# Where the running rows of a gather-and-reduce loop live: SBUF before, a PSUM bank after

## The chip, the cores and the metric

The kernel runs on one core of one Trainium2 chip. The metric is the device time of one launch in microseconds. Five engines work side by side, each through its own queue in order: PE (TensorE, matrix products; PEld are its weight loads), DVE (VectorE), ACT (ScalarE), POOL (GpSimd) and SP, which only issues DMAs. A gather of rows from HBM is issued by POOL, as one indirect DMA of 128 rows.

## The reference, cut to what matters

Two layers of a graph network on 3125 nodes of 256 numbers. Each layer adds, to the nodes' features, an edge part and an attention-like mixing, and then a mixture of experts. The edge part of the first layer takes a maximum over a node's incoming edges, that of the second a sum over messages that were made beforehand, one table for each of 8 relations:

```python
def _L0_gnn_ref(x, src, dst, theta_w, theta_b, phi_w, phi_b):
    theta_x = (x[dst] - x[src]) @ theta_w.T + theta_b
    e = jax.nn.relu(theta_x + x[src] @ phi_w.T + phi_b)
    return jax.ops.segment_max(e, dst, num_segments=x.shape[0])
...
def _L1_gnn_ref(node_feats, src, dst, edge_types, basis, comp, loop_w, h_bias, ln_gamma, ln_beta):
    W = jnp.einsum('rb,bio->rio', comp, basis)
    h_all = jnp.einsum('ni,rio->nro', node_feats, W)
    agg = jax.ops.segment_sum(h_all[src, edge_types], dst, num_segments=node_feats.shape[0])
    h = jax.nn.gelu(agg + node_feats @ loop_w + h_bias + node_feats, approximate=False)
    ...
x = x + _L0_gnn_ref(xn, ...) + _L0_mix_ref(xn, ...)
x = x + _L0_ffn_ref(_layernorm(x), ...)
x = x + _L1_gnn_ref(xn, ...) + _L1_mix_ref(xn, ...)
x = x + _L1_ffn_ref(_layernorm(x), ...)
```

What matters here: for every node, the rows of its neighbours are fetched from a table and reduced, by `max` in the first layer and by addition in the second.

## The kernel before, in words

**Tiles.** The nodes are sorted by their number of edges and lie in 25 tiles of 128. Tile `t` needs `STEPS[t]` rows for each of its nodes (45 for tile 0, 22 for tile 24, 814 in all); row `k` of a tile is one gather of 128 table rows, one for each partition. The source has a preparation, a fast path (`fast`) and a general path that this input doesn't take.

**The stages.** Up to about 100 us the edge lists are sorted and the first table, `btab`, is made. In the first edge pass (to about 1380 us) POOL gathers rows of `btab` (264 numbers: 256 and 8 of bookkeeping) and VectorE takes maxima, while PE and ACT do the mixing of the first layer, until line 1840, and then the first layer's sums, norms and experts. From 1380 to 1640 us the second table `htab_f` is made by 200 wide products. In the second edge pass (to about 2910 us) POOL gathers from `htab_f`, VectorE adds, and PE and ACT do the second layer's attention and its eight experts. Tiles 15 to 18 are `EARLY`: their rows are begun while the table is made and added into `sums` (lines 2140 and 2587), so that the second pass's `edge_pass` has 21 tiles with 696 rows.

**Order.** `edge_pass` (line 1335) writes out the order of VectorE and POOL by hand: after each chunk of rows it takes jobs from a list `bg`, so many units of cost for a row. A job's VectorE part stands in VectorE's queue at that place, and everything behind it waits with it. PE and ACT are not ordered by hand: a planner orders their instructions by what they need.

**The rows before.** In the first pass (`pairs`), the first two rows of a tile go straight into a tile `run` of two rows in SBUF, of which there are two (line 1634). The other rows go, by chunks of 3 or 4, into buffers `gt` (six, line 1714), and after every second row one addition-like operation of 512 numbers takes the pair into `run` (line 1368). Line 1643 saves the bookkeeping numbers of each chunk, line 1393 takes the maximum of `run`'s two halves into `acc`. In the second pass the chunks of 3 or 4 rows go into `gt` (five buffers, line 2012), a tree inside the chunk reduces them to one row (line 1375, first 512 wide, then 256), and line 1377 adds it to `acc`. `acc` begins as the node's own row, which SP loads from `otab` or POOL gathers (lines 2556 to 2561), one tile ahead. All operands of lines 1368, 1375, 1377 and 1393 are in SBUF.

**PSUM.** Four banks are `mm` (`ps_mm`), two belong to `ps_tr`, two to `ps_acc` (tags `acc1` and `acc2`). `ps_tr` serves transposes: a tile's features (line 183), the attention's keys (2268), and in each group of the second pass the two halves of the states (2394), the router's logits (2402, in the same pool) and the weights (2421). ACT copies each out (2270, 2395, 2423), but the logits are read by VectorE (2410). `acc2` holds the mixing's accumulator `pkv` (line 1757) until line 1829 reads it, then a column sum `pmean` (line 1881, which takes `acc1` and `acc2` in turn), and in the second pass the attention's accumulator and the experts' outputs.

**A group of the second pass** (`Group`, line 2310): sums, GELU, two norms in four steps `states_a` to `states_d` that go to and fro between VectorE and ACT, then `routes_a` (transposes and logits), the router's top two, then the experts, whose outputs VectorE takes at line 2482.

Of the kernel before, what the change touches and what calls it, by code (L numbers as in the profile page):

```python
# [99 lines left out]

@with_exitstack
def gps_kernel(ctx: ExitStack, tc: tile.TileContext, a, out):
# [8 lines left out]
    ps_tr = ctx.enter_context(tc.tile_pool(name="ps_tr", bufs=2, space=PSUM))  # L111
# [1207 lines left out]
    def fast():  # L1319
# [15 lines left out]
        def edge_pass(gp, table, wide, idx, op, bg, after, groups, most, pace, own, acc_of, aside, seen=None):  # L1335
# [4 lines left out]
            for g, tiles in enumerate(groups):  # L1340
                accs = []
                left = sum(STEPS[t] for t in tiles)
                for t in tiles:
                    acc = acc_of(t)
                    ids = idx(t)
                    pairs = own is None
                    two = acc[:, :, :D] if pairs else None
                    first = 2 * pairs

                    def fetch_row(dst, k):  # L1350
                        gather(dst, table, ids[:, U - 2 - k : U - 1 - k])

                    if pairs:
                        for k in range(2):
                            fetch_row(acc[:, 1 - k, :], k)
                        seen(t, 0, 0, 2, acc)
                    for i, (k0, k1) in enumerate(chunks(STEPS[t] - first, most)):
                        k0, k1 = k0 + first, k1 + first
                        m = k1 - k0
                        gw = gp.tile([P, most, wide], F32, name="gt")  # L1360
                        gt = gw[:, :, :D]
                        if pairs:
                            for a in range(k0, k1, 2):
                                b = min(a + 2, k1)
                                for k in range(a, b):
                                    fetch_row(gw[:, k1 - 1 - k, :], k)
                                d = two[:, : b - a, :]
                                V.tensor_tensor(d, d, gt[:, k1 - b : k1 - a, :], op=op)  # L1368
                            seen(t, i + 1, k0, k1, gw)
                        else:  # L1370
                            for k in range(k0, k1):
                                fetch_row(gw[:, k1 - 1 - k, :], k)
                            while m > 1:
                                h = m // 2
                                V.tensor_tensor(gt[:, :h, :], gt[:, :h, :], gt[:, m - h : m, :], op=op)  # L1375
                                m -= h
# [1314 lines left out]
```

## Time and profile before

| what | us |
|---|---|
| three timed executions: lowest, median, highest | 2953.78, 2956.93, 2958.68 |
| the profiled execution | 2956.36 |
| its span | 2954.5 |
| PE, weight loads, VectorE, ACT, POOL busy | 1868.2, 1201.3, 1227.5, 556.2, 1718.8 |
| gathers of the first pass into `gt` | 764 x 984 ns |
| gathers of the second pass into `gt` | 742 x 981 ns |
| line 1368, two rows into `run` | 364 x 690 ns, 36 x 425 ns |
| line 1375, the tree | 150 x 683 ns, 214 x 425 ns |
| line 1377, into `acc` | 182 x 428 ns |
| line 2395, ACT's copy of transposed states | 24, median 561 ns |
| mean clock granted to PE | 0.766 |

The span is the profiled execution from its first instruction to its last; the time of a run has a little around it. A line of the timeline gives start, duration, engine, source line, operation, the tiles written and read, and in brackets how long the engine had been idle and what ended that. A line of waits gives who waited for whom, the total in us, how often, and the longest. In a line of groups the two numbers behind the bar are busy time in us and the mean of one in ns, then the engine's idle time before. PE's records are modelled at their ends, and "another core or an unknown queue" is a wait whose releaser the profile couldn't name.

### The profile page before, as it was taken

What the parts mean: (1) busy time and instruction counts of PE and PEld (TensorE: products, weight loads), DVE (VectorE), ACT (ScalarE), POOL (GpSimd) and SP (SyncE); (2) the same over time, 40 slices, a digit from 0 to 9 for tenths busy, and PEclk for the clock granted to TensorE, in tenths of its full rate; (3) what the DMA queues carried; (4) which work ended last, traced back from release to release, by engine and by line L of the source; (5) the groups of instructions that cost most, each with busy time, mean ns of one, the idle gap of its engine ahead of it and who ended that gap; (6) DMA issues with size and microseconds to landing.
All of it is one profiled execution on the core that took longest, in us unless ns stands there. A gap on an engine that the chain in (4) does not pass through costs nothing.

```text
span 2954.5 us, 21207 instructions
## 1 busy us (share of the span) xinstructions
PE 1868.2 (63%) x6161; PEld 1201.3 (41%) x6161; DVE 1227.5 (42%) x3400; ACT 556.2 (19%) x1308; POOL 1718.8 (58%) x1830
## 2 busy tenths in 40 slices
PE   4345666413574635374998267858886886766868
PEld 2223333202342313243443145645554565554657
DVE  7434434434433424334664243335343434343342
ACT  5212221001110101022221122122111122122233
POOL 5566666675667566653146645655666555665651
PEclk9667767655686657687998668878897887887979
DMA  6533333343334233332357432322332222232320
GB/s 180 135 91 86 94 85 104 94 108 101 90 87 107 74 90 85 92 78 58 148 211 237 135 97 75 91 80 84 89 92 85 84 82 79 82 89 73 86 72 18
DMA packets 125963, 290.10 MB, mean 98 GB/s; under 512 B 41386, under 2 KB 63982, under 8 KB 122632
## 3 DMA queue, kind: packets, MB, share of 16 engines
q0 software_dynamic: 83184, 230.02, 28.4%
q1 hardware_dynamic: 38122, 55.88, 5.6%
q10 hardware_dynamic: 4526, 2.71, 0.3%
q8 instruction: 52, 0.85, 0.1%
q14 instruction: 79, 0.65, 0.1%
HBM read 249.07 MB, written 39.41 MB: 98 GB/s over the span
## 4 chain that ended last, share of the span: by engine, by line
PE 25%; issue 9%; another core or an unknown queue 7%; DVE 5%; POOL 4%; ACT 2%; DMA 1%; ACTq 0%; DVEq 0%; SPq 0%; POOLq 0%
PE mm L2432 9%; PE py L2463 7%; PE mm L189 6%; POOL gt L194 4%; DVE gt L1375 1%; PE mm L2326 1%; DVE bnst L163 1%; PE pctx L2271 0%; PE mm L2324 0%; DVE x L2482 0%; PE py L2449 0%; PE pt L2402 0%; DMA gt<-htab_f,idx2g 0%; DVE acc L1377 0%
## 5 line engine op out<-in xcount | busy, mean ns | idle before, releaser
L194 POOL DMA_INDIRECT gt<-htab_f,idx2g x742 | 727.8, 981 | 497.2 <-DVE acc L1377 241.3
L194 POOL DMA_INDIRECT gt<-btab,idx x764 | 751.6, 984 | 389.5 <-issue 208.5
L2432 PE MATMUL mm<-xT,w 128*128 128x256 f32 (+4 forms) x1536 | 429.8, 434 | 107.4 <-issue 61.2
L2463 PE MATMUL py<-w,hT 128*128 128x256 f32 (+1 forms) x1600 | 407.8, 407 | 71.6 <-issue 45.5
L2432 PEld LDWEIGHTS mm<-xT,w 128*128 128x128 f32 x1536 | 294.5, 217 | 224.1 <-issue 121.9
L2463 PEld LDWEIGHTS py<-w,hT 128*128 128x128 f32 (+1 forms) x1600 | 319.8, 203 | 144.1 <-issue 78.9
L1368 DVE TENSOR_TENSOR run<-run,gt 128x512 f32<-128x512 f32 (+1 forms) x400 | 266.3, 666 | 169.6 <-DMA gt<-btab,idx 110.8
L2436 ACT ACTIVATE hT<-mm,b 128x256 f32<-128x256 f32 (+4 forms) x384 | 174.9, 476 | 584.9 <-remote 266.3
L2482 DVE SCALAR_TENSOR_TENSOR x<-py,wf,x 128x256 f32<-128x256 f32 x200 | 88.1, 477 | 440.0 <-remote 226.0
L1375 DVE TENSOR_TENSOR gt<-gt 128x512 f32<-128x512 f32 (+1 forms) x364 | 193.5, 531 | 14.2 <-DMA gt<-htab_f,idx2g 4.9
L1555 PE MATMUL mm<-w,hT 128*128 128x256 f32 x400 | 130.0, 471 | 106.2 <-issue 85.8
L189 PE MATMUL mm<-w_rel,xT 128*128 128x512 f32 x400 | 179.0, 605 | 7.1 <-issue 3.2
L1526 PE MATMUL mm<-xT,w 128*128 128x384 f32 (+2 forms) x320 | 113.8, 519 | 72.8 <-ACT y L1566 34.8
L1555 PEld LDWEIGHTS mm<-w,hT 128*128 128x128 f32 x400 | 90.6, 234 | 158.6 <-issue 123.9
L189 PEld LDWEIGHTS mm<-w_rel,xT 128*128 128x128 f32 x400 | 75.9, 193 | 102.2 <-issue 89.9
L1526 PEld LDWEIGHTS mm<-xT,w 128*128 128x128 f32 x320 | 69.4, 242 | 116.2 <-ACT y L1566 38.4
L1886 PE MATMUL pmean<-ones,xt 128*128 128x1 f32 (+1 forms) x100 | 21.3, 317 | 139.2 <-DVE xt L172 133.7
L189 PE MATMUL mm<-w_qkv,xT 128*128 128x512 f32 (+1 forms) x200 | 90.9, 579 | 25.7 <-issue 19.2
L194 POOL DMA_INDIRECT gt<-htab_f,soon x72 | 71.6, 995 | 44.7 <-issue 20.9
L189 PE MATMUL pt<-w_own,xT 128*128 128x256 f32 x100 | 42.0, 553 | 70.7 <-issue 37.0
L194 POOL DMA_INDIRECT run<-btab,idx x50 | 48.7, 973 | 64.2 <-DVE idx L1630 30.9
L1886 PEld LDWEIGHTS pmean<-ones,xt 128*128 128x128 f32 (+1 forms) x100 | 21.9, 300 | 148.3 <-DVE xt L172 140.9
(440 smaller groups left out, 2221.9 us busy)
## 6 DMA issues: line engine op xcount, KB each, us to landing
htab_f<-hs SPq DMA_DIRECT2D x25, 1024.0 KB
gt<-btab,idx POOLq DMA_INDIRECT x764
gt<-htab_f,idx2g POOLq DMA_INDIRECT x742
w<-in_f_W_dram SPq DMA_DIRECT2D x20, 512.0 KB
ntab<-x SPq DMA_DIRECT2D x5, 640.0 KB
btab<-bs SPq DMA_DIRECT2D x5, 640.0 KB
x<-in_x_dram SPq DMA_DIRECT2D x4, 640.0 KB
otab<-xn SPq DMA_DIRECT2D x16, 128.0 KB
```

What stands on the lines that cost most here:

```text
L163: V.bn_stats(out=st, in_=src)
L189: PE.matmul(ps, lhs[:, c, t * P : (t + 1) * P], w[:, c, :], start=start and c == 0, stop=stop and c == 1)
L194: G.indirect_dma_start(out=dst, out_offset=None, in_=table, in_offset=bass.IndirectOffsetOnAxis(ap=idx, axis=0))
L1368: V.tensor_tensor(d, d, gt[:, k1 - b : k1 - a, :], op=op)
L1375: V.tensor_tensor(gt[:, :h, :], gt[:, :h, :], gt[:, m - h : m, :], op=op)
L1526: PE.matmul(ph[:, :n], w1[:, i, c, f * P : (f + 1) * P], xT[:, c, at0 : at0 + n], start=(c == 0), stop=(c == 1),)
L1555: PE.matmul(py[:, i * D : (i + 1) * D], hTs[i][:, f, j * P : (j + 1) * P], w2[:, i, f, :], start=False, stop=(f == FC - 1), skip_group_che ...
L1886: PE.matmul(pmean[0][:, c : c + 1], xt_tok[:r, t, c * P : (c + 1) * P], ones[:r, 0:1], start=(t in (1, SEEN + 1) and c == 0), stop=(t in ( ...
L2432: PE.matmul(ph[:, :n], w1s[e][:, c, f * P : (f + 1) * P], xT[:, c, at0 : at0 + n], start=(c == 0), stop=(c == 1),)
L2436: S.activation(hT[:, f, :n], ph[:, :n], AF.Gelu, bias=b1[:, e, f : f + 1])
L2463: PE.matmul(py[:r, j * D : (j + 1) * D], hT[:, f, at : at + r], w2s[e][:, f, :], start=(f == 0), stop=(f == FC - 1),)
L2482: V.scalar_tensor_tensor(d, y, wf[:r, t, e : e + 1], d, op0=ALU.mult, op1=ALU.add)
```

## The change

The running rows go to PSUM. In the first pass, once the mixing is done, `run` is a tile of two rows in `acc2`, the bank of the mixing's accumulator; until then it stays in SBUF. In the second pass `run` is in the second of the two banks of `ps_tr`, and everything that used `ps_tr` turns to the first one alone: a small class `Turns` hands out the two tags in turn, and `k` is set to 1 before the second pass and back to 2 behind it. Since `acc2` is taken, both column sums `pmean` use `acc1`.

Both passes now reduce in the same way. All rows go into chunks of at most four (the first may be shorter so that pairs come out even), each pair is taken into `run` by one operation of 512 numbers, which reads `run` in PSUM and the pair in SBUF, and the last pair's result goes to a tile `ends` in SBUF. In the first chunk the pairs are taken together, and an odd row is copied. In the second pass the node's own row and the first gathered row share a tile `begun`, which counts as a pair. The final operation adds the halves of `ends` into `acc`.

```diff
@@ -98,6 +98,16 @@
     return list(zip(at, at[1:]))
 
 
+class Turns:
+
+    def __init__(self, pool):
+        self.pool, self.k, self.n = pool, 2, 0
+
+    def tile(self, shape, dtype, name):
+        self.n += 1
+        return self.pool.tile(shape, dtype, name=name, tag=f"tr{self.n % self.k}")
+
+
 @with_exitstack
 def gps_kernel(ctx: ExitStack, tc: tile.TileContext, a, out):
     nc = tc.nc
@@ -108,7 +118,7 @@
     small = ctx.enter_context(tc.tile_pool(name="small", bufs=6))
     work = ctx.enter_context(tc.tile_pool(name="work", bufs=2))
     ps_mm = ctx.enter_context(tc.tile_pool(name="ps_mm", bufs=4, space=PSUM))
-    ps_tr = ctx.enter_context(tc.tile_pool(name="ps_tr", bufs=2, space=PSUM))
+    ps_tr = Turns(ctx.enter_context(tc.tile_pool(name="ps_tr", bufs=1, space=PSUM)))
     ps_acc = ctx.enter_context(tc.tile_pool(name="ps_acc", bufs=1, space=PSUM))
@@ -1332,7 +1342,7 @@
         comp = bcast_load("comp", a["comp"], 4 * NX, ek)
         br = bcast_load("br0", a["f0_br"], NX, ek)
 
-        def edge_pass(gp, table, wide, idx, op, bg, after, groups, most, pace, own, acc_of, aside, seen=None):
+        def edge_pass(gp, table, wide, idx, op, bg, after, groups, pace, acc_of, run_of, aside, seen=None):
 
 
             credit = 0.0
@@ -1341,56 +1351,46 @@
                 accs = []
                 left = sum(STEPS[t] for t in tiles)
                 for t in tiles:
-                    acc = acc_of(t)
+                    begun, ends = acc_of(t)
                     ids = idx(t)
-                    pairs = own is None
-                    two = acc[:, :, :D] if pairs else None
-                    first = 2 * pairs
-
-                    def fetch_row(dst, k):
-                        gather(dst, table, ids[:, U - 2 - k : U - 1 - k])
-
-                    if pairs:
-                        for k in range(2):
-                            fetch_row(acc[:, 1 - k, :], k)
-                        seen(t, 0, 0, 2, acc)
-                    for i, (k0, k1) in enumerate(chunks(STEPS[t] - first, most)):
-                        k0, k1 = k0 + first, k1 + first
-                        m = k1 - k0
-                        gw = gp.tile([P, most, wide], F32, name="gt")
-                        gt = gw[:, :, :D]
-                        if pairs:
-                            for a in range(k0, k1, 2):
-                                b = min(a + 2, k1)
-                                for k in range(a, b):
-                                    fetch_row(gw[:, k1 - 1 - k, :], k)
-                                d = two[:, : b - a, :]
-                                V.tensor_tensor(d, d, gt[:, k1 - b : k1 - a, :], op=op)
-                            seen(t, i + 1, k0, k1, gw)
-                        else:
-                            for k in range(k0, k1):
-                                fetch_row(gw[:, k1 - 1 - k, :], k)
-                            while m > 1:
-                                h = m // 2
-                                V.tensor_tensor(gt[:, :h, :], gt[:, :h, :], gt[:, m - h : m, :], op=op)
-                                m -= h
-                            V.tensor_tensor(acc, own(t) if i == 0 else acc, gt[:, 0, :], op=op)
+                    run = run_of()
+                    n, own = STEPS[t], begun is not None
+                    odd = (n + own) % 2
+                    cuts_ = [0] + list(range(4 - odd - own, n, 4)) + [n]
+                    for i, (k0, k1) in enumerate(zip(cuts_, cuts_[1:])):
+                        gw = gp.tile([P, 4, wide], F32, name="gt")
+
+                        def rows_of(a, b):
+                            return gw[:, k1 - b : k1 - a, :D]
+
+                        for k in range(k0, k1):
+                            dst = begun[:, 1, :] if own and k == 0 else gw[:, k1 - 1 - k, :]
+                            gather(dst, table, ids[:, U - 2 - k : U - 1 - k])
+                            if i and (k - k0) % 2:
+                                V.tensor_tensor(ends if k == n - 1 else run, run, rows_of(k - 1, k + 1), op=op)
+                        if i == 0:
+                            if odd:
+                                one = begun if own else rows_of(0, 2)
+                                V.tensor_tensor(run[:, 0, :], one[:, 0, :], one[:, 1, :], op=op)
+                                V.tensor_copy(run[:, 1, :], rows_of(k1 - 1, k1)[:, 0, :])
+                            else:
+                                V.tensor_tensor(run, begun if own else rows_of(0, 2), rows_of(k1 - 2, k1), op=op)
+                        if seen is not None:
+                            seen(t, i, k0, k1, gw)
                         if t == 0 and i == 3:
-                            d = two[: P // 2, 0, :] if pairs else acc[: P // 2, :]
+                            d = run[: P // 2, 0, :]
                             V.tensor_tensor(d, d, spill, op=op)
 
                         rate = min(max(sum(c for c, _ in bg) / left, pace[0]), pace[1])
-                        n1 = k1 - (k0 if i else 0)
-                        left -= n1
-                        credit = min(credit, 0.0) + rate * n1 if bg else 0.0
+                        left -= k1 - k0
+                        credit = min(credit, 0.0) + rate * (k1 - k0) if bg else 0.0
                         aside()
                         while bg and credit > 0.0:
                             cost, job = bg.popleft()
                             job()
                             credit -= cost
-                    if pairs:
-                        acc = accp.tile([P, D], F32, name="acc")
-                        V.tensor_tensor(acc, two[:, 0, :], two[:, 1, :], op=op)
+                    acc = accp.tile([P, D], F32, name="acc")
+                    V.tensor_tensor(acc, ends[:, 0, :], ends[:, 1, :], op=op)
                     if t == NT - 1:
 
                         pj = ps_mm.tile([P, 512], F32, name="mm")
@@ -1631,7 +1631,14 @@
 
             def begin0(t):
                 rows_asked(t)
-                return l0w.tile([P, 2, ROW], F32, name="run", bufs=2)
+                return None, l0w.tile([P, 2, D], F32, name="ends")
+
+            mixed = []
+
+            def run0():
+                if mixed:
+                    return ps_acc.tile([P, 2, D], F32, name="run", tag="acc2")
+                return l0w.tile([P, 2, D], F32, name="run")
 
             places = l0w.tile([P, U], F32, name="places")
             G.iota(places, pattern=[[-1, U]], base=0, channel_multiplier=0, allow_small_or_imprecise_dtypes=True)
@@ -1839,6 +1846,7 @@
                 yield
                 V.tensor_copy(u_mix, pu.rearrange("p (m d) -> p m d", m=2))
                 m0x.close()
+                mixed.append(True)
                 begin()
@@ -1878,7 +1886,7 @@
                     V.reciprocal(self.rs[:, : self.k], self.rs[:, : self.k])
                     for j, t in enumerate(self.tiles):
                         if t in (1, SEEN + 1):
-                            pmean[0] = ps_acc.tile([P, 2], F32, name="pmean", tag=f"acc{1 + (t > 1)}")
+                            pmean[0] = ps_acc.tile([P, 2], F32, name="pmean", tag="acc1")
                         normalize(xt_tok[:, t, :], x[:, t, :], self.mv[:, j, :], self.rs[:, j : j + 1])
                         V.tensor_tensor(x[:, t, :], x[:, t, :], bet, op=ALU.add)
                         r = rows(t)
@@ -1954,8 +1962,8 @@
 
             with tc.manual_schedule(engines={mybir.EngineType.DVE, mybir.EngineType.Pool}):
                 edge_pass(
-                    gp, btab[:], ROW, idx1.get, ALU.max, bg, after0, GROUPS, 4, (0.9, 1.3), None,
-                    begin0, ahead, seen0,
+                    gp, btab[:], ROW, idx1.get, ALU.max, bg, after0, GROUPS, (0.9, 1.3),
+                    begin0, run0, ahead, seen0,
                 )
                 while bg:
                     bg.popleft()[1]()
@@ -2212,6 +2220,7 @@
                 w1s[e] = mat_load(f"w1_{e}", a["f1_W1"][e], pool, F, nc.sync)
                 w2s[e] = mat_load(f"w2_{e}", a["f1_W2"][e], pool, D, nc.sync)
 
+            ps_tr.k = 1
             kx = ExitStack()
             kp = kx.enter_context(tc.tile_pool(name="kp", bufs=1))
             w1qkv = mat_load("w1qkv", a["m1_qkv"], kp, 3 * P, nc.sync)
@@ -2554,17 +2563,20 @@
             inits, order1 = {}, [t for tiles in GROUPS1[2:] for t in tiles]
 
             def load_init(t):
-                inits[t] = accp.tile([P, D], F32, name="acc")
+                inits[t] = fin.tile([P, 2, D], F32, name="begun", bufs=2)
                 if t in owns:
-                    gather(inits[t], h_rows, own_i[:, t : t + 1])
+                    gather(inits[t][:, 0, :], h_rows, own_i[:, t : t + 1])
                 else:
-                    nc.sync.dma_start(inits[t], otab[t * P : (t + 1) * P, :])
+                    nc.sync.dma_start(inits[t][:, 0, :], otab[t * P : (t + 1) * P, :])
 
             def begin1(t):
                 i = order1.index(t) + 1
                 if i < len(order1):
                     load_init(order1[i])
-                return inits[t]
+                return inits[t], fin.tile([P, 2, D], F32, name="ends")
+
+            def run1():
+                return ps_tr.pool.tile([P, 2, D], F32, name="run", tag="tr1")
 
             def first_groups():
@@ -2600,11 +2612,12 @@
                 first_groups()
                 edge_pass(
                     gp, h_rows, D, lambda t: idx2[:, t, :], ALU.add, bg, lambda g, *a: after1(g + 2, *a),
-                    GROUPS1[2:], 4, (0.9, 1.3), lambda t: inits[t], begin1, aside,
+                    GROUPS1[2:], (0.9, 1.3), begin1, run1, aside,
                 )
                 while bg:
                     bg.popleft()[1]()
                     flush()
+        ps_tr.k = 2
         fx.close()
 
     unfit = nc.values_load(flag[0:1, 0:1])
```

## The prediction

> **What bounds the kernel now.** I read the totals and the chain of waits first, then windows cut where the passes begin and end, then the waits of each engine inside them, then the timeline around single gathers. The windows:
>
> ```profile
> core 0: us, PE busy (x) PEld busy (x) DVE busy (x) ACT busy (x) POOL busy (x), PEclk, DMA share, GB/s
> 100.00:491.00 391.00, 210.38 (x578) 108.84 (x578) 157.40 (x539) 82.03 (x305) 254.56 (x259) 0.71 0.36 95
> 491.00:1380.00 889.00, 435.21 (x1240) 262.08 (x1241) 341.77 (x921) 86.02 (x185) 568.29 (x579) 0.67 0.35 92
> 1380.00:1640.00 260.00, 217.55 (x550) 102.23 (x548) 147.78 (x388) 52.68 (x118) 104.78 (x106) 0.92 0.55 190
> 1640.00:2912.00 1272.00, 929.06 (x3419) 667.98 (x3420) 504.13 (x1307) 272.96 (x541) 743.99 (x758) 0.81 0.29 82
> ```
>
> 491 us is where the mixing ends (the copy of line 1840); only after it does the change put the first pass's running rows in PSUM. A gather takes 0.95 us and leaves 0.30 before the next, so 579 of them need 724 of the 889 us: no engine is full in the first pass, but POOL is nearest. In the second pass (1640 to 2912) PE works 929 us of 1272. The waits say which of two engines is late:
>
> ```profile
> DVE run L1368 <- DMA gt<-btab,idx: 110.8, 65, 2.9
> POOL gt L194 <- DVE slots L1643: 55.8, 13, 11.4
> ...
> DVE gt L1375 <- DMA gt<-htab_f,idx2g: 4.9, 2, 3.1
> POOL gt L194 <- DVE acc L1377: 241.3, 49, 12.5
> PE pt L2394 <- DVE hh L172: 60.5, 9, 13.7
> PE pt L2402 <- ACT xT L2395: 39.9, 8, 15.0
> ```
>
> In the first pass VectorE waits for rows 65 times, and at other times POOL waits for a buffer (17 idle stretches over 0.45 us after 491 us, 149 us together). In the second VectorE hardly waits for a row, while POOL stands 241 us behind line 1377: a faster gather has almost nobody waiting for it there.
>
> What the change touches on POOL is seen where a gather starts inside an addition:
>
> ```profile
> 1020.87 0.69 DVE L1368 TENSOR_TENSOR run<-run,gt 128x512 f32<-128x512 f32 x1 [2.45 <-remote]
> 1021.10 1.27 POOL L194 DMA_INDIRECT gt<-btab,idx  x1 [0.30 <-issue]
> 1022.68 0.95 POOL L194 DMA_INDIRECT gt<-btab,idx  x1 [0.30 <-issue]
> ...
> 2679.82 0.88 DVE L2482 SCALAR_TENSOR_TENSOR x<-py,wf,x 128x256 f32<-128x256 f32 x2 [1.33 <-PE py L2463]
> 2680.01 0.95 POOL L194 DMA_INDIRECT gt<-htab_f,idx2g  x1 [0.30 <-issue]
> ```
>
> The gather at 1021.10 is held until the addition with two SBUF inputs ends at 1021.56, and takes 1.27 us. The one at 2680.01 starts inside an operation whose other tensor lies in PSUM, in the operand order that the change uses, and takes 0.95. Gather by gather, what is above 0.945 us comes to 22.2 us after the mixing, 15.1 of it (73 gathers) beside line 1368, and to 26.0 us in the second pass, 18.4 beside lines 1375 and 1377.
>
> **The change part by part.** (1) Relief of the gathers: 15.1 us of POOL time in the first pass, 18.4 in the second. How much reaches the end? In the first pass, the gathers that VectorE waits for: 65 waits of two rows, 130 of 578, 22%: 3.4 us. In these stretches an addition starts 0.4 us into a gather and is over before the next, so the held gathers lie mostly where VectorE catches up and POOL later waits anyway. In the second pass the chain has 3.5% of the span (103 us of 1272, 8%) on gathers: 1.5 us. Bounds: nothing, or all of it in the first pass. **-5 us**.
>
> [...]
>
> (2) Run-ahead in the first pass: before, the first two rows of a tile go into a tile of their own (two such), beside six buffers; after, every row passes through the six. A buffer holds 3.82 rows before (764 in 200) and 3.80 after (814 in 214). A stall's run-ahead of about 23 rows crosses a tile's start 0.7 times (32.6 rows a tile), so POOL stands still 0.7 x 2 x 1.25 = 1.75 us earlier in each of 17 stalls, 30 us, of which the same 22% counts: **+7**. Bounds 0 and 30.
>
> (3) VectorE's work: in the second pass 150, 214 and 182 operations (102.5 + 91.0 + 78.0 = 271.5 us) become by the cuts 333 of 512 elements at 0.690, 30 of 256 at 0.425 and 9 copies at about 0.42 (an estimate from the 256-wide row): 246 us. The chain holds 42.7 us of lines 1375 and 1377, 16% of their work, so 25 us less is **-4**. Bounds 0 and -25. In the first pass 315.5 us become 318; nothing, hidden by the 200 us and more that VectorE waits for PE and ACT.
>
> The price of a PSUM operand: these rows have their tensors in SBUF (1368, 1375) and one in PSUM (2474):
>
> ```profile
> L1368 DVE TENSOR_TENSOR run<-run,gt 128x512 f32<-128x512 f32 x364 | 251.1, 690 | 158.4 <-DMA gt<-btab,idx 108.6 <-remote 26.4 <-DVE run L1368 8.4
> L1375 DVE TENSOR_TENSOR gt<-gt 128x512 f32<-128x512 f32 x150 | 102.5, 683 | 5.1 <-DMA gt<-htab_f,idx2g 4.9
> L2474 DVE TENSOR_TENSOR x<-x,py 128x512 f32<-128x512 f32 x9 | 6.2, 687 | 24.1 <-PE py L2449 18.0 <-PE py L2463 6.1
> ```
>
> Reading costs nothing. VectorE never writes PSUM here: bounds by the slowest and fastest 512-wide rows, 751 ns (line 1584) and 497 (line 1580), +61 and -193 on some 600 operations, +37 and -116 us, at 16% +6 and -19. I take 690, since the nearest row differs by memory only.
>
> [...]
>
> (4) One transposing bank in the second pass. Line 2394 transposes a group's two halves into two banks and ACT copies each (line 2395, median 0.56 us) while PE goes on. With one bank the second half's transposes wait for the first copy, and the logits of line 2402, in the same bank, for the second: two copies in series with PE, 1.1 us and two hand-overs, 1.2 a group. PE waits at line 2402 for ACT in 8 of the 12 groups: **+10**. Lower bound 0, other matmuls being put between. Upper: in three groups (ended at 2226.8, 2500.6, 2610.0) the chain has 20.5, 15.3 and 10.9 us between the states and ACT's copy, with PE out of work; were each repeated by the added hand-over, +47. The 25 transposes of line 2268 run in pairs, 1.76 us for two tiles. With one bank a tile costs 0.27 + 0.37 + 0.05 if the next transpose goes ahead of the product, as now, or 0.27 + 0.37 + 0.56 = 1.2 if not: between 0 and 0.32 x 25 = 8, **+4**, on the chain throughout.
>
> (5) Nothing: both column sums in acc1 (the second waits for the guess's copy of the first, which line 1448 awaits anyway; without that cover, the 23.0 us PE waits there). The own rows go into two `begun` buffers in place of `acc`, free once the tile before has done its first addition; SP's and POOL's loads keep their place in the queues. The single `run` and `ends` are touched by VectorE alone, in order, so nobody queues behind them.
>
> Sum: -5 + 7 - 4 + 10 + 4 = **+12 us** on the profiled execution's 2956.4 (span 2954.5 and 1.9 around it, 0.6 below the runs' median): **2968 us**.
>
> **Rivals.** *The relief reaches the end:* POOL is nearest to full in the first pass, and a chain there would pass all 15.1 us on; with VectorE's 4 and 1.5, and the bank and run-ahead hidden, 2956.4 - 21 = **2936**. Against it: 241 us of POOL waiting. *It cancels:* the planner, which orders PE and ACT itself, puts other matmuls between the halves: -5 + 7 - 4 = -2, **2955**. *The bank runs PE dry:* term 4 at +47 in place of +10, **3005**, decided once PE has no queued matmul at three or more of the hand-overs. *The lock stays:* the gathers remain long, the change not doing what it is built for: 2968 + 5 = **2973**; the row at 2680.01 speaks against it.
>
> **How the numbers follow.** Chances: +12 as summed 0.36, relief 0.32, cancelling 0.16, PE dry 0.11, lock 0.05. A measurement here can tell 0.2%, 6 us. Slower is the first, fourth and fifth less 0.04 of the first that falls within 6 us: 0.48; same 0.16 + 0.04 = 0.20; faster 0.32. The likeliest's own range, terms 1 to 3 each moved half way to their bounds (-8 to +28 in all), is 2948 to 2984; for 8 in 10 it reaches to the relief on one side and most of the way to PE dry on the other: 2930 to 2996.
>
> **What would show it.** Gathers of the first pass after the mixing near a mean of 0.955 us (now 0.982) show the relief; POOL's idle before them growing shows the run-ahead; additions at 690 ns the PSUM price; line 2394 waiting for ACT about once a group the bank. A second pass shorter than 1272 us by over 10 makes term 4 wrong, a first pass shorter by over 10 terms 1 and 2.

## The result, and the profile after

| | lowest, median, highest us |
|---|---|
| before, 6 runs | 2943.35, 2952.01, 2958.68 |
| the change, 6 runs | 2971.44, 2987.45, 3008.82 |

The change is slower: its time is 1.0128 of the time before, 95% interval 1.0096 to 1.0159, or 38 us (28 to 47). The forecast was +12 us, 2968, with a range of 2930 to 2996. The direction and the range hold; the size is three times the forecast. The profiled execution took 2983.25 us, its span is 2981.4, 26.9 more than before.

The windows of the changed kernel, cut at the same events as those before (the end of the mixing, the last gather of the first pass, and 18 us after the first gather of the second pass); the columns are as there:

```profile
100.00:479.00 379.00, 213.89 (x576) 112.99 (x577) 159.33 (x540) 82.08 (x305) 253.85 (x257) 0.71 0.37 97
479.00:1396.00 917.00, 427.72 (x1223) 252.85 (x1221) 344.07 (x908) 82.94 (x179) 557.86 (x581) 0.66 0.34 90
1396.00:1662.00 266.00, 224.84 (x561) 107.47 (x560) 147.36 (x388) 53.69 (x121) 102.93 (x106) 0.91 0.51 176
1662.00:2938.00 1276.00, 931.62 (x3433) 665.31 (x3434) 484.38 (x1137) 278.18 (x545) 728.40 (x758) 0.81 0.29 84
```

By this one execution the first pass after the mixing lost 28 us (889 to 917), the table 6, and the second pass only 4 (1272 to 1276). In the second pass PE and ACT are busy 3 and 5 us more than before, VectorE and POOL 20 and 16 less: no engine has much more work, so what is lost is idle time. A second profile of the same kernel put the loss elsewhere (experiment 1), so the split of one execution is not to be trusted here.

The groups of the changed kernel, by line and shape (busy us, mean ns, idle before):

```profile
L1370 DVE TENSOR_TENSOR run<-run,gt 128x512 f32<-128x512 f32 x639 | 445.2, 697 | 135.5 <-DMA gt<-btab,idx 49.9 <-remote 42.5 <-issue 18.6
L1370 DVE TENSOR_TENSOR ends<-run,gt 128x512 f32<-128x512 f32 x46 | 31.7, 689 | 18.8 <-DMA gt<-btab,idx 7.3 <-DMA gt<-htab_f,idx2g 5.0 <-issue 2.5
L204 POOL DMA_INDIRECT gt<-btab,idx x814 | 789.0, 969 | 481.4 <-issue 222.5 <-DVE slots L1650 121.4 <-DVE idx L1630 73.1
L204 POOL DMA_INDIRECT gt<-htab_f,idx2g x721 | 693.4, 962 | 508.0 <-issue 193.4 <-DVE run L1370 189.0 <-DVE sums L2599 45.3
```

Two things were as forecast. An operation with its running rows in PSUM takes 697 ns and not 690. And the gathers are no longer held: 981 ns became 962 in the second pass; in the first, the gathers after the mixing go from 983 to 961 (the 969 includes those before it). What was not forecast is that the time grew although both of these rows are right.

### The profile page after: what moved, and what is told of

Read it like the earlier page. It is cut to its first block, busy times and chain, and to the rows that moved or that the text cites. A ratio compares the mean times of both kernels' runs of the same rounds, so it can differ in the third digit from the quotient of the medians.

```text
span 2981.4 us, 21020 instructions
## 1 busy us (share of the span) xinstructions
PE 1878.4 (63%) x6161; PEld 1201.0 (40%) x6161; DVE 1211.5 (41%) x3218; ACT 557.8 (19%) x1308; POOL 1690.2 (57%) x1830
## 4 chain that ended last, share of the span: by engine, by line
PE 27%; issue 8%; another core or an unknown queue 7%; DVE 6%; ACT 2%; POOL 1%; DMA 0%; ACTq 0%; DVEq 0%; POOLq 0%
PE mm L2441 9%; PE py L2472 8%; PE mm L199 6%; DVE run L1370 2%; PE pctx L2280 1%; POOL gt L204 1%; DVE bnst L173 1%; DVE x L2491 1%; PE py L2458 1%; ACT hT L2445 0%; PE pt L2411 0%; PE mm L2335 0%; PE pt L2403 0%; DVE x L2376 0%
## 5 line engine op out<-in xcount | busy, mean ns | idle before, releaser
L204 POOL DMA_INDIRECT gt<-btab,idx x814 | 789.0, 969 | 481.4 <-issue 222.5
L204 POOL DMA_INDIRECT gt<-htab_f,idx2g x721 | 693.4, 962 | 508.0 <-issue 193.4
L1370 DVE TENSOR_TENSOR run<-run,gt 128x512 f32<-128x512 f32 x639 | 445.2, 697 | 135.5 <-DMA gt<-btab,idx 49.9
L2472 PE MATMUL py<-w,hT 128*128 128x256 f32 (+1 forms) x1600 | 411.9, 406 | 109.1 <-issue 64.2
L2441 PE MATMUL mm<-xT,w 128*128 128x256 f32 (+4 forms) x1536 | 418.6, 427 | 82.4 <-ACT hT L2445 34.7
L1526 PE MATMUL mm<-xT,w 128*128 128x384 f32 (+2 forms) x320 | 130.2, 570 | 193.8 <-issue 94.3
L1555 PE MATMUL mm<-w,hT 128*128 128x256 f32 x400 | 108.7, 428 | 12.5 <-issue 10.7
L1555 PEld LDWEIGHTS mm<-w,hT 128*128 128x128 f32 x400 | 83.0, 214 | 49.9 <-issue 35.0
L194 ACT COPY xT<-pt 128x256 f32<-128x256 f32 x100 | 36.2, 375 | 282.5 <-issue 142.2
L1876 DVE TENSOR_TENSOR acc<-acc,pt 128x256 f32<-128x256 f32 x25 | 10.4, 417 | 173.2 <-PE pt L199 115.4
L2403 PE MATMUL pt<-ident,hh 128*128 128x128 f32 x50 | 15.6, 402 | 85.7 <-DVE hh L182 33.4
```

The costliest lines, as they stand in the source:

```text
L194: S.copy(xT[:, :, t * P : (t + 1) * P], pt)
L204: G.indirect_dma_start(out=dst, out_offset=None, in_=table, in_offset=bass.IndirectOffsetOnAxis(ap=idx, axis=0))
L1370: V.tensor_tensor(ends if k == n - 1 else run, run, rows_of(k - 1, k + 1), op=op)
L1526: PE.matmul(ph[:, :n], w1[:, i, c, f * P : (f + 1) * P], xT[:, c, at0 : at0 + n], start=(c == 0), stop=(c == 1),)
L1555: PE.matmul(py[:, i * D : (i + 1) * D], hTs[i][:, f, j * P : (j + 1) * P], w2[:, i, f, :], start=False, stop=(f == FC - 1), skip_group_che ...
L2441: PE.matmul(ph[:, :n], w1s[e][:, c, f * P : (f + 1) * P], xT[:, c, at0 : at0 + n], start=(c == 0), stop=(c == 1),)
```

## The experiments

Ratios are to the kernel before, timed in turn with it on the same chip. Experiments 1 to 4 ran on one chip, 5 to 8 on a second, 9 and 10 on a third, 11 and 12 on a fourth; where two kernels of different chips are compared, it is by their ratios. "Second pass" below, where a length is given for it, means the time from line 2300 of the changed kernel (the attention's last product, on VectorE) to the last addition into `x`, in the one profiled execution of each.

**1. The change again.** No edit.

> The changed kernel, unaltered, for a second profile and more times. The sum of the prediction (one transposing bank and run-ahead as the costs): about 2987 us, and the second pass (from the first of its gathers to the end) longer than before by 10 us or more. The regrouping theory (the new cuts of the chunks move VectorE's jobs, and the order of PE and ACT with them; memory has no part in it): about 2987 us, and again 20 to 40 us more than before between the end of the mixing and the last gather of the first pass, with the second pass within 5 us of before.

2999.19 us, 1.0192 (1.0148 to 1.0237). The loss is real, but its place moved: between the end of the mixing and the last gather of the first pass this profile has 896 us, against 917 in the first one and 887 before. The regrouping theory, formed after the first profile, expected 20 to 40 us there in every execution; it has 9.

**2. Running rows of the first pass back in SBUF.**

```diff
-                if mixed:
-                    return ps_acc.tile([P, 2, D], F32, name="run", tag="acc2")
                 return l0w.tile([P, 2, D], F32, name="run")
```

> The changed kernel with the running rows of the first pass in SBUF throughout; VectorE's, POOL's and ACT's instructions in the same order. The sum of the prediction: the gathers of the first pass are held again (mean 983 ns in place of 961), of which 3.4 us reach the end: 2990 us. Relief in full: 2999. If writing PSUM from VectorE, or the bank taken from the column sums, cost the time: 2955 to 2965. The regrouping theory: 2987, within 5 us.

2987.50 us, 1.0119 (1.0069 to 1.0169). The first pass's gathers are held again, as expected (mean 988 ns after the mixing). Most of the loss is still there: 35 us, of 57 in experiment 1, which ran on the same chip, and of 38 in the result.

**3. Running rows of the second pass back in SBUF, and two transposing banks.**

```diff
-            ps_tr.k = 1
...
-                    run = run_of()
+                    run = run_of() or ends
...
-                return ps_tr.pool.tile([P, 2, D], F32, name="run", tag="tr1")
+                return None
```

> The changed kernel with the running rows of the second pass in SBUF (in the tile that holds the last pair) and both transposing banks back in turn. The sum of the prediction: 14 us less for the bank and 1.5 more for the gathers: 2974. The bank running PE dry: 2940 to 2950. The regrouping theory: 2987, within 5 us.

2956.96 us, 1.0014 (0.9974 to 1.0054). The loss is gone but for 4 us (-8 to 16), so most of it belongs to the second pass's half of the change.

**4. Both passes in SBUF.** Edits 2 and 3 together; VectorE's and POOL's instructions stand in the same order as in the changed kernel.

> The changed kernel with the running rows of both passes in SBUF and both transposing banks: what is left is the new cuts of the chunks, the pairs, the lost tiles for the first rows. The sum of the prediction: run-ahead +7 and VectorE's lesser work -4, 2955. The regrouping theory: 2980 to 2995, all of the loss without any PSUM.

2930.85 us, 0.9965 (0.9931 to 0.9999): a little faster than before. The regrouping theory falls here. The new cuts, the pairs, `begun` and both column sums in `acc1` are all in this kernel, and together they cost nothing. Between this kernel and experiment 3 lies only the memory of the first pass's rows: 0.0049, or 14 us for rows in PSUM, with intervals that touch.

**5. The kernel before with one transposing bank in its second pass.**

```diff
+            ps_tr.k = 1
             kx = ExitStack()
```

(with the class `Turns` from the change).

> The kernel before with one transposing bank in its second pass and nothing else. The sum of the prediction: +14 us, 2964. If the bank is what makes the second pass of the changed kernel longer: +40 or more, 2990. If it is the memory of the running rows instead: within 5 us of before.

2966.06 us, 1.0034 (1.0001 to 1.0067), +10 us. This is the bank as the prediction summed it (+14), and far from the 40 that would explain the result.

**6. Both passes in SBUF, one bank.** Experiment 4 with `ps_tr.k = 1` kept.

> The changed kernel with the running rows of both passes in SBUF, but one transposing bank in the second pass: between it and e3_both_sbuf (2931 us) lies the bank alone, between it and e1_run0_sbuf (2987) the memory of the rows alone. Bank: 2970 to 2990. Memory of the rows: 2928 to 2940. Both by halves: about 2958.

2948.93 us, 0.9987 (0.9959 to 1.0015). The bank costs 0.0022 against experiment 4 (6.5 us; 18 by the medians). From here to experiment 2 (1.0119, on the other chip) it is 0.0132, 39 us; with experiment 4, which shares experiment 2's chip, it is 0.0154 for bank and rows together, 45 us. Between these two kernels VectorE, POOL and SP have the same instructions in the same order, and PE and ACT differ in four places where a few of the experts' instructions change order: what differs is that the second pass's running rows lie in PSUM. The new order doesn't explain the loss: at the first of the four places experiment 2 has already lost 32 of the 44 us that it loses from the start of the second pass on (and 38 of 44 in the pair of experiments 10 and 9 below, which differs in the same places).

The timeline shows where the bank's part is. The attention's transposes, two banks (experiment 4), then one (this one); start, duration, engine and line, tiles, count, idle before:

```profile
1684.22 0.38 PE L2274 MATMUL pt<-ident,kT 128*128 128x128 f32 x2
1684.59 0.62 ACT L2276 ACTIVATE ks<-pt,rs 128x128 f32<-128x128 f32 x2 [1.02 <-PE pt L2274]
1685.02 1.13 PE L2277 MATMUL pctx<-x,ks 128*128 128x256 f32 x4 [0.41 <-ACT ks L2276]
```

```profile
1683.82 0.42 PE L2275 MATMUL pt<-ident,kT 128*128 128x128 f32 x1
1684.34 0.37 ACT L2277 ACTIVATE ks<-pt,rs 128x128 f32<-128x128 f32 x1 [1.59 <-PE pt L2275]
1684.76 1.22 PE L2278 MATMUL pctx<-x,ks 128*128 128x256 f32 x2 [0.52 <-ACT ks L2277]
1685.78 0.42 PE L2275 MATMUL pt<-ident,kT 128*128 128x128 f32 x1
```

With two banks a pair of tiles goes through together; with one, each tile takes its own turn, 1.95 us in the median. Against experiment 4 this stage (first transpose to last product) is 11.3 us longer here, between 10.8 and 12.0 in the change, in experiment 1 and in experiment 2, and 13.0 and 37.5 in experiments 9 and 10 (the latter stage began 20 us earlier); in those with the change's order and two banks it is the same to 0.1. The groups' transposes (the other user of the bank) added little: 1193.7 us for the second pass against 1188.4 here, 1225.1 against 1225.2 in experiment 5.

**7. Rows of the second pass in PSUM, but transposes turning between two banks again.** Experiment 2 with

```diff
-                        pt = ps_tr.tile([P, 512], F32, name="pt")
+                        pt = (ps_mm.tile([P, 512], F32, name="mm") if c else ps_tr.tile([P, 512], F32, name="pt"))
...
-                pt = ps_tr.tile([P, 2, P], F32, name="pt")
+                pt = ps_mm.tile([P, 2, P], F32, name="mm") if t % 2 else ps_tr.tile([P, 2, P], F32, name="pt")
```

> e1_run0_sbuf (rows of the second pass in PSUM, 2987 us) with every second transpose of the attention and the second half of a group's states in a bank of ps_mm, so that transposes turn between two banks again. Bank: 2940 to 2960. Memory of the rows: 2980 to 2990.

2962.09 us, 1.0033 (1.0006 to 1.0060): between the two expectations. By the ratios it gives 25 us back against experiment 2 and stays 20 above experiment 4. Both parts are there; neither is the whole. (The edit also puts transposes into the banks of `mm`, and PE's order differs from experiment 4's in some 20 places, so this pair is less clean than the one before.)

**8. Five row buffers in the first pass in place of six.** Experiment 4 with `bufs=5`.

> e3_both_sbuf (2931 us) with five row buffers in the first pass in place of six: 3.8 rows of run-ahead less. By the prediction's term 2 (1.4 rows lost cost 7 us): 17 stalls x 3.8 rows x 1.25 us x 22% = +18 us, 2949. If run-ahead isn't worth anything in the first pass: 2926 to 2936.

2942.60 us, 0.9934 (0.9900 to 0.9968). A whole buffer less, 3.8 rows, costs nothing that can be measured: experiment 4, on the other chip, has 0.9965, and the intervals overlap. (Against this kernel, on its own chip, experiment 7 is 0.0099 slower, 29 us.) Run-ahead is worth nothing here.

**9 and 10. POOL slowed down again.** After every second gather of the second pass, a memset of one column, in experiment 2 (rows in PSUM) and in experiment 6 (rows in SBUF):

```diff
                             gather(dst, table, ids[:, U - 2 - k : U - 1 - k])
+                            if own and k % 2:
+                                G.memset(spare, 0.0)
```

> e1_run0_sbuf (rows of the second pass in PSUM, one bank, 2987 us) with a memset of 128x1 on POOL after every second gather of the second pass, 0.09 us each, some 350 of them: POOL gets back about the 28 us that the shorter gathers saved it; VectorE's, PE's, ACT's and SP's instructions keep their order. If the loss comes from POOL's shorter gathers (rows earlier, and what that collides with): back to 2949 or little more. If it comes from VectorE's operand in PSUM itself: 2985 to 3000.

> e5_sbuf_one_bank (rows in SBUF, one bank, 2949 us) with the same memsets: what the memsets cost by themselves. By the 441 us that POOL waits for VectorE in the second pass: 2945 to 2955. If POOL's time counts in full: 2980.

With rows in PSUM 3028.54 us, 1.0218 (1.0182 to 1.0254); with rows in SBUF 2990.31, 1.0106 (1.0068 to 1.0145). So it isn't the shorter gathers that hurt: making POOL slow again did not bring the time back, it made it worse. And the pair, on one chip, repeats the distance of experiments 6 and 2: 0.0112, 33 us, for rows in PSUM. The second finding was expected by nobody: 342 memsets of 118 ns, 40 us of POOL time, cost 29 us with rows in PSUM (against experiment 2) and 35 with rows in SBUF (against experiment 6), by ratios from different chips, although POOL waits long for VectorE in this pass (180.5 us behind line 1370 in experiment 6, 212.2 in experiment 2). Either POOL's time counts nearly in full there, or the memsets disturb something else; no run tells these apart.

The second pass in all these profiles (a count from the traces, us):

```
kernel                         second pass  PE busy  PE idle  POOL busy
before                              1225.2    931.6    293.6      704.9
5  before, one bank                 1225.1    938.3    286.9      707.3
4  SBUF, two banks                  1188.4    927.9    260.5      717.0
8  SBUF, two banks, 5 buffers       1201.8    928.0    273.8      719.4
3  SBUF, two banks, PSUM in first   1209.2    925.9    283.3      714.9
6  SBUF, one bank                   1193.7    921.4    272.3      716.0
10 SBUF, one bank, memsets          1219.3    930.9    288.4      757.5
7  PSUM, two banks                  1225.6    934.4    291.1      688.6
2  PSUM, one bank                   1237.2    933.9    303.4      688.5
   the change                       1221.7    923.0    298.7      690.8
1  the change again                 1230.1    927.8    302.3      690.7
9  PSUM, one bank, memsets          1263.6    938.0    325.6      728.6
```

Of the kernels with the change's cuts and pairs (all but the first two of the table), every one with rows in SBUF and no memsets is below 1210, every one with rows in PSUM above 1220, though POOL saves 28 us of gathers in the latter. PE's work is the same to 2%; its idle time grows. The operations next to the rows don't tell why: VectorE's operation ends and POOL's gather starts 0.270 us later in both (median of the waits for the row operation), an ACT operation of 128x256 (the experts' hidden layer) takes 471 to 472 ns in all of them, and the matmuls of the experts' second product start 0.216 us apart at the full clock and 0.427 at half of it (medians), beside a running-row operation or not, in experiments 6 and 2 alike. The windows of the second pass in experiments 6 and 2, one fence each, give the same:

```profile
1735.00:2929.00 1194.00, 922.34 (x3524) 669.94 (x3523) 473.60 (x1131) 275.06 (x544) 716.00 (x719) 0.84 0.29 84
```

```profile
1737.00:2974.00 1237.00, 933.58 (x3519) 679.38 (x3519) 474.17 (x1130) 273.96 (x544) 688.61 (x720) 0.83 0.28 81
```

VectorE 474 us in both, POOL 27 less, PE 11 more at a clock of 0.83 in place of 0.84, and 43 us more in all. What does differ is the place of the idle time. The clock granted to PE is either 1.0 or 0.5 in the records. Matmul by matmul, experiment 2 loses 206 us against experiment 6 at those that only it meets at the half clock, regains 193 at those that only the other meets so, and loses 26 at the rest. A stretch at the half clock looks like this one of the changed kernel's PE timeline, with the window around it:

```profile
2113.78 0.59 PE L2472 MATMUL py<-w,hT 128*128 128x256 f32 x1 [2.31 <-issue]
2115.18 0.58 PE L2472 MATMUL py<-w,hT 128*128 128x256 f32 x1 [0.81 <-issue]
2116.59 0.58 PE L2472 MATMUL py<-w,hT 128*128 128x256 f32 x1 [0.82 <-issue]
2118.68 0.58 PE L2472 MATMUL py<-w,hT 128*128 128x256 f32 x1 [1.51 <-issue]
2121.48 0.59 PE L2472 MATMUL py<-w,hT 128*128 128x256 f32 x1 [2.22 <-issue]
```

```profile
2111.00:2135.00 24.00, 7.38 (x12) 3.55 (x13) 0.43 (x1) 2.06 (x3) 15.50 (x17) 0.51 0.33 97
```

Matmuls that elsewhere follow each other after 0.216 us, or 0.427 at the half clock, start 1.40, 1.41, 2.09 and 2.80 us apart, all near multiples of 0.70. No releaser is shown for these waits ("issue"), but the granted clock is low: 0.51 over the stretch. Of such starts (a wait of the kind "issue", at least 1.35 us after the matmul before, within 0.02 of a multiple of 0.70) the changed kernel's profile has 87, 69 of them wholly at the half clock; before has 60 and 47.

Do they explain the loss? In the second pass these starts take 83 us in experiment 2 against 79 in 6, 113 in 7 against 96 in 4, and 121 in 9 against 77 in 10; the time at the half clock is 429 us against 385, 420 against 406, and 445 against 428. The losses of the three pairs are 43, 37 and 44 us. Neither count gives all three, so by what rows in PSUM cost time stays open. The last two runs, on another chip, show what a profile without such starts looks like.

**11. The kernel before with only the first pass's rows in PSUM,** in its own order, with its own tile for the first rows:

```diff
-                                d = two[:, : b - a, :]
-                                V.tensor_tensor(d, d, gt[:, k1 - b : k1 - a, :], op=op)
+                                w = b - a
+                                src = (two if a == first else run)[:, :w, :]
+                                d = (two if b == STEPS[t] else run)[:, :w, :]
+                                V.tensor_tensor(d, src, gt[:, k1 - b : k1 - a, :], op=op)
```

(`run` is a tile in `acc2` once the mixing is done, and `two` until then; the column sums are both in `acc1`.)

> The kernel before with its first pass's running rows in the mixing's bank once the mixing is done: a tile's first pair is read from the tile in SBUF and written to PSUM, the last pair's result goes back to SBUF; both column sums in acc1. Chunks, buffers, own tile for the first rows and the order of all engines stay as before, and the second pass is untouched. The prediction's term 1 (relief, 15.1 us of POOL time, 22% of it reaching the end): 3 us faster, within 0.2% of before. Relief in full: 15 us faster. If rows in PSUM cost as in the second pass (some 0.13 us for each of the operations, of which there are some 270 after the mixing): 25 to 45 us slower.

**12. The kernel before with the pairs in its second pass only,** rows in SBUF, two banks: experiment 4's second pass behind the first pass of before.

> The kernel before with the pairs, the new cuts and begun in its second pass only, rows in SBUF, two transposing banks: the change's second pass without PSUM, behind the first pass of before. If what makes e3_both_sbuf and e8_five_buffers faster than before (0.9965 and 0.9934 of it) lies in the second pass alone, as their second passes of 1284 and some 1295 us against 1324 say: 0.990 to 0.995 of before. By the prediction's term 3: 4 us, 0.9986.

These two ran on another chip than all others, and there the kernel before takes 2454.86 us (2451.32 to 2459.46, 18 runs) in place of some 2955. On it, experiment 11 takes 2446.63 us, 0.9967 (0.9955 to 0.9978): rows in PSUM in the first pass are 8 us faster (5 to 11). Experiment 12 takes 2449.59 us, 0.9977 (0.9968 to 0.9986), 6 us faster.

The profile of experiment 11 is another world. Its groups:

```profile
L194 POOL DMA_INDIRECT gt<-btab,idx x764 | 737.9, 966 | 232.7 <-issue 192.2
L194 POOL DMA_INDIRECT gt<-htab_f,idx2g x742 | 729.1, 983 | 227.6 <-issue 196.8
L2469 PE MATMUL py<-w,hT 128*128 128x256 f32 (+1 forms) x1600 | 379.6, 392 | 45.4 <-DVE x L2488 45.4
L1380 DVE TENSOR_TENSOR gt<-gt 128x512 f32<-128x512 f32 (+1 forms) x364 | 194.8, 535 | 266.3 <-DMA gt<-htab_f,idx2g 253.7
```

and its waits after the mixing:

```profile
DVE runp L1373 <- DMA gt<-btab,idx: 334.4, 208, 2.8
```

POOL's idle time is its own 0.30 us between gathers and little else; VectorE waits 334 us for rows in the first pass and 254 in the second, where the trace of before had 110.8 and 4.9. No wait of this execution is put down to an unknown releaser, and the matmuls of line 2469 have no idle time of the kind "issue" (64.2 us for the same line in the changed kernel's profile). The clock of this chip is another, too; the spans and mean clocks of experiment 11 and of the kernel before in its first profile:

```profile
core 0: 2443.3 us, clock 0.829
core 0: 2954.5 us, clock 0.766
```

Experiment 11 spends 835 us at the half clock and 1608 at the full one, before on its own chip 1382 and 1573: the 511 us between them lie in the time at the half clock. Experiments 11 and 12 have none of the starts on the grid of 0.70 us, though they too run a third of their time at the half clock. On this chip POOL is at a gather or in the 0.30 us behind it nearly all the time: in experiment 11 its 555 instructions from 400 to 1100 us and the 0.30 behind each make 698 of the 700 us (531 of them busy), and the 794 from 1360 to 2400 us make 1020 of 1040 (782 busy). Shorter gathers paid about in full in its first pass (8 us, 5 to 11, for the 7 counted below). The new cuts and pairs of the second pass pay as well; by what isn't shown, since VectorE, whose work they lessen, waits for rows there (297.5 us in experiment 12). The gathers of the first pass after the mixing average 960 ns here and 973 in experiment 12, which has its rows in SBUF: 554 x 13 ns are 7 us, and 8 were gained. The changed kernel itself was not run on this chip. Whether it is faster there is open.

Of the kernels tried, those of experiments 8 and 4 were the fastest on the slower chips (0.9934 and 0.9965 of before, intervals that overlap, against 1.0128 and 1.0192 for the change), and those of experiments 11 and 12 were the two tried on the faster one (0.9967 and 0.9977).

## Why the prediction was right in sign and wrong in size

**The relief of the gathers (-5).** The mechanism is right: the mean fell to 961 and 962 ns in the two passes, near the 955 that the prediction asked for. Its worth was read from POOL's waits: 241 us of waiting, so "a faster gather has almost nobody waiting for it". That reading is weak. Experiments 9 and 10 charged most of 40 us of POOL time to the end (if a memset costs nothing else), and experiment 11 passed about all of 7 us on, on a chip where POOL does not wait. On the slower chips the relief can't be seen: with the first pass's rows in PSUM the kernel was 14 us slower, not faster (experiments 4 and 3, intervals that touch).

**Run-ahead (+7).** Wrong: nothing that shows. The term counted with 1.4 rows less of run-ahead in each stall; experiment 8 took 3.8 rows away, nearly three times as much, and lost nothing (9 us less by the ratios, give or take 14, against the 18 that the term would give). So a share of POOL's stalls can't be priced here by the share of gathers that VectorE waits for.

**VectorE's lesser work (-4).** Right in sign; -10 (-20 to 0) for all new cuts and pairs of both passes in experiment 4, -6 (-8 to -3) for the second pass alone in experiment 12. That VectorE's time is what was saved isn't shown.

**The price of a PSUM operand (0).** This is the step that failed. "I take 690, since the nearest row differs by memory only": the row was right, 697 ns, and with it the bound of +6 was kept. But the price doesn't stand in the row's duration. With the same order of VectorE and POOL, rows of the second pass in PSUM cost 39 us (experiments 6 and 2), 33 (10 and 9) and 20 (4 and 7, with two banks), net of the gathers that they shorten. The prediction bounded an operation's price by the durations of other operations; it had no term for what such an operation does to the others. The mechanism by which it does so isn't shown. That it has to do with the half clock and the starts on the grid of 0.70 us is a conjecture: there the kernels drift apart, but neither count gives the loss in all three pairs; and on the chip without such starts rows in PSUM were a gain, but in the first pass of another kernel, so that the two were never compared on one chip.

**One bank (+14).** The sum was right: +10 (0 to 20) in experiment 5, +6.5 in experiment 6. The split was not. The attention took +11 in place of +4: the next transpose does not go ahead of the product, and a tile costs 1.95 us, beyond the 1.2 that the upper bound allowed. (25 tiles at 1.95 in place of 0.88 would be 27 us more; the stage grew by 11. With two banks three of its steps take 6.2, 10.6 and 10.0 us in the trace of before, with PE idle for 3.3, 6.8 and 7.5 of them; that one bank hides most of this idle time is an estimate, from the 27 and the 11.) The twelve groups took 0 to 5 in place of 10. PE does wait there as forecast, about once a group:

```profile
PE pt L2403 <- ACT xT L2404: 28.8, 10, 18.0
```

But these waits hardly lengthen the pass: experiment 6 has them too (10 times, 9.1 us), and its second pass is 5 us longer than that of experiment 4, where two profiles of one kernel differ by 8 (the change and experiment 1).

**Nothing for `pmean`, `begun` and `ends`.** Experiment 4 contains all three and isn't slower than before.

**The sum** of what was measured: -10 (new cuts and pairs) + 39 (rows of the second pass, beside one bank) + 6.5 (bank) + 3 to 22 (rows of the first pass, experiment 2 against the change's two ratios) = 38 to 57, against 38 and 57 for the two sets of the change; each step begins where the one before ends, so the sum must come out, and it is no independent proof. Of the rivals, "the lock stays" (2973) and "the bank runs PE dry" (3005) lie 14 and 18 us from the result, nearer than the forecast's 19, and both for a wrong reason: the gathers were freed, and the bank cost less than its sum. "The relief reaches the end" is what the other chip shows for the first pass. That the result lies in the stated range is luck: the likeliest's own range (2948 to 2984) misses it, and the wider one held it by reaching towards "PE dry", which did not happen.

## What to carry to other kernels

In this kernel an operation's own duration didn't price where it reads and writes (697 ns against 690, but 20 to 39 us for the pass): put back one memory at a time, with the order of the queues unchanged, before believing a row that "costs the same". Where a profile has much idle time without a releaser, its shares can say little about what a microsecond of an engine is worth (here POOL had 241 us of waiting in the second pass, and 40 us more of its time cost 29 and 35): look at the granted clock in those stretches, and slow that engine by a known amount. And this kernel took 2454.86 us on one chip and 2950 to 2963 on three others, so a change should be timed on more than one.

## What the runs showed of the hardware that was not expected

- The kernel before takes 2454.86 us on one chip and 2950 to 2963 on three others, with medians that repeat. The slower ones have stretches in which PE starts matmuls at multiples of 0.70 us in place of 0.216 or 0.427 (87 such starts in the changed kernel's profile, 69 of them at the half clock), and waits without a known releaser (252 us of VectorE's in the second pass of experiment 6); the profiles of experiments 11 and 12 have neither. The mean clock granted to PE was 0.829 and 0.830 in its two profiles, against 0.754 to 0.770, and the difference in time lies in the time at the half clock (835 us against 1382).
- A held gather is seen with two SBUF inputs, not only in tensor_tensor: the gathers that began inside a scalar_tensor_tensor of the shape 128x512 (the combination of `w_rel`) took 1198 ns on average before (9) and 1200 in the changed kernel (8), and those that began inside one of 128x256 with a PSUM operand (`x<-py,wf,x`) 949 (49) and 948 (42).
- A memset of 128x1 on POOL took 118 ns between gathers.
